# Reciprocal deviation by way of DRAM, and zeros' matmuls at the launch, in an RWKV block

## The chip, the cores and the metric

One core of a Trainium2 chip runs the whole program in one launch. The metric is the device time of that launch in microseconds, the median of several runs.

## The reference

An RWKV block with f32 data on 8 sequences of 256 tokens with 512 channels (32 heads of 16). Cut to what matters:

```
xn = ln(x, ln1_w, ln1_b);  sx = shift(xn) - xn            # shift: the row before, first row from the state
xxx = tanh((xn + sx*maa_x) @ maa_w1)                      # 5 groups of 32
x5  = xn + sx * (maa_stack + xxx @ maa_w2)                # 5 mixed inputs
w   = exp(-exp(time_decay + tanh(x5[1] @ decay_w1) @ decay_w2))
r, k, v = x5[3] @ Wr.T, x5[0] @ Wk.T, x5[2] @ Wv.T;  g = silu(x5[4] @ Wg.T)
for t in tokens:                                          # state s: 16 x 16 per head
    a = k_t v_t^T;  out_t = r_t (u*a + s);  s = a + w_t * s
att = (out - mean) * rsqrt(var + eps) * gn_w + gn_b       # per head of 16 channels
x   = x + (att * g) @ Wo.T
xn2 = ln(x, ln2_w, ln2_b);  sx2 = shift(xn2) - xn2
x   = x + sigmoid((xn2 + sx2*ffn_maa_r) @ Wr2.T) * (relu((xn2 + sx2*ffn_maa_k) @ Wk2.T)**2 @ Wv2.T)
```

## The kernel before

Channels lie on the 128 partitions and tokens along the row; a tile of 128 x 2 x 256 holds half of the 512 channels (`q` is 0 or 1). Each of the 8 batches goes through three functions. `inputs_of_scan` normalizes x, transposes it on TensorE, and makes w, k, v, r and g. `scan` runs the recurrence: v goes to DRAM (`vo`) and is read back in an order that repeats it over partitions (`vs`, line 874), VectorE multiplies it by k (883) and scans (885), GpSimd multiplies by r (888), and TensorE sums over the 16 rows of a state (`gather`, 896). `rest` normalizes per head, multiplies by g, and does the Wo product, the second norm and the feed-forward part.

In `rest` the variance comes out of a TensorE product with a mean matrix (`pv`, 922): the four channel blocks of 128 lie on four groups of 32 partitions, and 32 rows hold the 8 heads of a block, each four times. ScalarE takes the root (927), VectorE the reciprocal (929): `rs`, 128 x 256. Each block's 32 rows must then stand on all four groups of 32 partitions of `att`'s layout. For that ScalarE makes 16 copies of 32 x 256 per batch (lines 948 to 952), into `sqs[1]` (the tile `sq`) for q = 0 and into a tile of the pool `rk` for q = 1. GpSimd multiplies `att` by them (953), ScalarE applies gn_w and gn_b (957), GpSimd multiplies by g (962), and TensorE takes the Wo product. The last batch does the copying with TensorE instead (`psr`, 937).

The launch: x of batch 0 is loaded first, VectorE makes its statistics and the normalized rows (562), TensorE transposes them with the identity `idt` (588), VectorE writes xn from PSUM (595), and ScalarE writes xn * (1 - maa_x) from the same PSUM tile (598), with scale and bias from `ow`, which four small GpSimd operations make in `owners` (517 to 524). VectorE adds the shifted part (622), and TensorE's product with `maa_w1` follows. Between them TensorE centers Wv (`centered_weights`).

The order of all work is written out by hand: `TURNS` gives each piece of each stage a rank, one row for the preparation, then eight rows each for the three functions. `Plan.order` takes pieces by rank as their inputs and buffers come free, gives each a planned start by its own table of costs, and emits the program in the order of these starts. So each engine's queue, and the queue of loads on SyncE (all `dma(...)` calls, line 390), is fixed when the program is built; an instruction at the head of a queue that has to wait holds what is behind it. A few stores are issued from ScalarE's queue (810 and 860).

Of the kernel before, what the change touches and what calls it, by code (L numbers as in the profile page):

```python
# [9 lines left out]
AF = mybir.ActivationFunctionType  # L10
ALU = mybir.AluOpType
# [56 lines left out]
class Plan:  # L68
# [46 lines left out]
    def stage(self):  # L115
# [225 lines left out]
def tile_rwkv_block(  # L341
# [73 lines left out]
    dw1, dw2 = const("dw1", [P, NK, DEC]), const("dw2", [2 * DEC, E])  # L415
    hm = const("hm", [P, NK, 32])
    eh = const("eh", [P, 4])
    ow = const("ow", [P, 2, NK])
    W = {n: [const(f"W{n}{h}", [P, 2, E]) for h in range(2)] for n in "kvrg"}

    pool("s0", 2, [P, NK, S])
# [693 lines left out]
```

## Time and profile before

| | |
|---|---|
| median of 3 runs | 615.86 us (615.41 to 616.64) |
| the profiled execution | 616.02 us, its span 614.2 us |
| TensorE busy | 593.8 us, 97% |
| VectorE, ScalarE, GpSimd busy | 546.0, 515.8, 522.3 us |
| bytes moved by DMA | 124.73 MB, 203 GB/s |
| granted clock of TensorE | 1.00 |

In the profile, L12 is line 12 of the kernel, and the helper `mul` (line 401) issues most matmuls, so that they are told apart by their tiles. Names are written out <- in. In a group of instructions stand the count, the busy time, the mean of one in ns, and the idle time of the engine before them with what ended it. In the timeline stand start, duration, engine, line, operation, tiles, shapes and count. In lists of waits stand the total, the number of times, and the longest. `SPq` and `ACTq` are the queues of SyncE and ScalarE that issue DMAs. A matmul's end is modelled, so TensorE's busy time includes some of its pipeline's tail.

### The profile page before, as it was taken

The page shows a single profiled execution, that of the slowest core. Times are in us where ns is not written, and L with a number is a line of the kernel's source. Part 1 is how long each engine was busy: PE and PEld are TensorE (multiplying, and loading weights), DVE is VectorE, ACT ScalarE, POOL GpSimd, SP SyncE. Part 2 cuts the span into 40 slices and gives each one's busy share as a digit, 9 for nine tenths or more (in the row PEclk, how much of TensorE's full clock was granted, in tenths as well). Part 3 has the DMA queues.
Part 4 walks back from the last instruction along what each step waited for, and adds up shares of the span by engine and source line. Part 5 has one row for each costly group of instructions (what it writes and reads, how often), then busy time and mean ns, then how long its engine had stood idle before and what let it go on. Part 6 is the DMA issues. An engine that isn't in the chain of part 4 may idle for free.

```text
span 614.2 us, 17191 instructions
## 1 busy us (share of the span) xinstructions
PE 593.8 (97%) x7068; PEld 345.9 (56%) x7068; DVE 546.0 (89%) x487; ACT 515.8 (84%) x1171; POOL 522.3 (85%) x421
## 2 busy tenths in 40 slices
PE   4899999899999999999999999999999999999997
PEld 4575656457544764357653885465644474456463
DVE  5789999999999989799898999999999999995432
ACT  4878878999999989999999798999899799966431
POOL 2799999999989999899978999999969998897030
PEclk9999999999999999999999999999999999999999
DMA  8887779568969777867777896796958698681551
GB/s 291 272 199 184 194 186 257 141 176 211 273 174 255 188 187 211 212 201 208 221 188 221 269 230 181 179 273 166 246 142 221 174 257 233 203 238 36 195 186 46
DMA packets 52493, 124.73 MB, mean 203 GB/s; under 512 B 5824, under 2 KB 11200, under 8 KB 52416
## 3 DMA queue, kind: packets, MB, share of 16 engines
q1 hardware_dynamic: 48048, 119.46, 71.2%
q10 hardware_dynamic: 4368, 4.20, 2.2%
q8 instruction: 55, 0.90, 0.7%
q14 instruction: 22, 0.18, 0.1%
HBM read 115.25 MB, written 8.39 MB: 201 GB/s over the span
## 4 chain that ended last, share of the span: by engine, by line
PE 73%; ACT 13%; POOL 5%; DVE 4%; issue 2%; DMA 1%; ACTq 0%; SPq 0%; POOLq 0%; DVEq 0%
PE ps L401 61%; PE ps L896 8%; PE ps L588 2%; ACT att L846 1%; PE ps L760 1%; POOL st L888 1%; ACT wrep L866 1%; POOL mix L720 1%; ACT sq L951 1%; ACT rk L951 1%; DVE st L885 1%; DMA idt<-in_consts 1%; ACT vs L876 1%; ACT att L957 1%; ACT L866 1%
## 5 line engine op out<-in xcount | busy, mean ns | idle before, releaser
L885 DVE TENSOR_TENSOR_SCAN st<-wrep,vs 128x1024 f32<-128x1024 f32 x128 | 289.5, 2280 | 4.1 <-ACT wrep L866 1.0
L888 POOL TENSOR_TENSOR st<-st,r 128x1024 f32<-128x1024 f32 x128 | 254.4, 2001 | 6.2 <-DVE st L885 5.7
L883 DVE TENSOR_TENSOR vs<-vs,ps 128x1024 f32<-128x1024 f32 x122 | 144.2, 1207 | 2.4 <-ACT vs L876 2.1
L401 PE MATMUL ps<-Ws,mix 128*32 128x512 f32 (+1 forms) x864 | 115.0, 589 | 0.8 <-ACT o L986 0.8
L401 PEld LDWEIGHTS ps<-Ws,mix 128*32 128x32 f32 (+1 forms) x864 | 37.4, 116 | 64.8 <-issue 56.9
L720 POOL TENSOR_TENSOR mix<-mix,xn 128x512 f32<-128x512 f32 x62 | 66.7, 1090 | 7.6 <-DVE mix L705 7.6
L896 PE MATMUL ps<-st,con 128*32 128x256 f32 x1024 | 61.6, 380 | 0.9 <-POOL st L888 0.4
L401 PE MATMUL ps<-mix,Wv 128*32 128x256 f32 (+1 forms) x748 | 60.0, 380 | 0.3 <-DVE mix L717 0.3
L401 PE MATMUL ps<-mix,Wr 128*32 128x256 f32 (+1 forms) x616 | 59.2, 380 | 0.6 <-ACT vs L876 0.6
L401 PE MATMUL ps<-mix,Wk 128*32 128x256 f32 (+1 forms) x856 | 58.5, 380 | 0.5 <-DVE x L968 0.3
L401 PE MATMUL ps<-mix,Wg 128*32 128x256 f32 (+1 forms) x712 | 58.6, 379 | 0.0
L401 PE MATMUL ps<-mix,Ws 128*32 128x256 f32 (+1 forms) x688 | 58.0, 380 | 0.0
L401 PE MATMUL ps<-Ws,g 128*32 128x512 f32 (+1 forms) x416 | 56.6, 593 | 0.3 <-POOL g L962 0.2
L610 POOL TENSOR_TENSOR sx<-xn 128x512 f32<-128x512 f32 x31 | 32.3, 1052 | 27.5 <-ACT xn L605 22.5
L635 POOL TENSOR_TENSOR mix<-mix,xn 128x512 f32<-128x512 f32 x44 | 47.6, 1098 | 5.0 <-ACT mix L633 3.8
L846 ACT COPY att<-ps 32x256 f32<-32x256 f32 x128 | 46.7, 365 | 4.4 <-PE ps L838 2.3
L703 ACT ACTIVATE ps<-ps,vec 128x256 f32<-128x256 f32 x112 | 46.8, 443 | 4.1 <-PE ps L401 2.7
L401 PEld LDWEIGHTS ps<-mix,Wv 128*32 128x32 f32 (+1 forms) x748 | 40.2, 120 | 16.9 <-issue 2.3
L401 PEld LDWEIGHTS ps<-mix,Wr 128*32 128x32 f32 (+1 forms) x616 | 40.6, 128 | 16.1 <-POOL mix L720 1.1
L401 PEld LDWEIGHTS ps<-mix,Ws 128*32 128x32 f32 (+1 forms) x688 | 39.9, 123 | 16.1 <-ACT mix L633 0.8
L896 PEld LDWEIGHTS ps<-st,con 128*32 128x32 f32 x1024 | 32.5, 110 | 28.0 <-POOL st L888 4.7
L401 PEld LDWEIGHTS ps<-mix,Wg 128*32 128x32 f32 (+1 forms) x712 | 39.0, 122 | 15.6 <-issue 0.3
(133 smaller groups left out, 968.0 us busy)
## 6 DMA issues: line engine op xcount, KB each, us to landing
vs<-vo SPq DMA_DIRECT2D x128, 512.0 KB, 5.5
Ws<-in_wo SPq DMA_DIRECT2D x16, 512.0 KB, 5.3
Ws<-in_fr SPq DMA_DIRECT2D x16, 512.0 KB, 6.3
Ws<-in_fk SPq DMA_DIRECT2D x16, 512.0 KB, 7.2
Ws<-in_fv SPq DMA_DIRECT2D x16, 512.0 KB, 4.9
x<-in_x SPq DMA_DIRECT2D x9, 512.0 KB, 6.5
vo<-v ACTq DMA_DIRECT2D x15, 256.0 KB, 4.6
out<-o SPq DMA_DIRECT2D x15, 256.0 KB, 4.4
```

Of the source, the lines that this page charges most:

```text
L401: nc.tensor.matmul(out[i : i + n], lhsT=w[:, i : i + n], rhs=x, start=first, stop=final)
L588: nc.tensor.transpose(ps()[:, m, n * P : (n + 1) * P], xh[n]()[:, k * P : (k + 1) * P], idt())
L610: take(512, [sx], [xn], lambda xn=xn, sx=sx, e=nc.vector if quick else nc.gpsimd: e.tensor_tensor(sx(), xn()[:, :, 0:T], xn()[:, :, 1 : T ...
L635: gp(512, t, [t, xn[q]], lambda q=q, t=t: nc.gpsimd.tensor_tensor(t(), t(), xn[q]()[:, :, 1 : T + 1], ALU.add))
L703: act(256, p_, [p_, vec], lambda g=g, q=q, m=m, p_=p_: nc.scalar.activation(p_()[:, m, :], p_()[:, m, :], AF.Identity, bias=col(f"maa_{g}" ...
L720: gp(512, t, [t, xn[q]], lambda q=q, t=t: nc.gpsimd.tensor_tensor(t(), t(), xn[q]()[:, :, 1 : T + 1], ALU.add))
L846: act(350, atts[q], [pc], lambda i=32 * (2 * q + m), m=m, q=q, h=32 * h: nc.scalar.copy(atts[q]()[h : h + 32, m, :], pc()[i : i + 32, 0, :]))
L866: act(4 * T, w, [ew], lambda m=m, w=w, ew=ew: nc.scalar.activation(w()[:, :, 1:T], ew()[:, m : m + 1, 0 : T - 1].to_broadcast([P, 4, T - 1 ...
L883: dve(4 * T, [vs], [vs, kp], lambda m=m, vs=vs, kp=kp: nc.vector.tensor_tensor(vs(), vs(), kp()[:, m : m + 1, :].to_broadcast([P, 4, T]), ...
L885: dve(4 * T, [st], [w, vs], lambda w=w, vs=vs, st=st: nc.vector.tensor_tensor_scan(st().rearrange("p n t -> p (n t)"), w().rearrange("p n ...
L888: gp(4 * T, st, [st, r], lambda m=m, st=st, r=r: nc.gpsimd.tensor_tensor(st(), st(), r()[:, m : m + 1, :].to_broadcast([P, 4, T]), ALU.mul ...
L896: nc.tensor.matmul(pat()[32 * i : 32 * i + 32, 0, :], lhsT=con()[:, s : s + 32], rhs=done[i]()[:, j, :], start=(j == 0), stop=(j == 3),)
```

## The change

Four things. In seven of the eight batches the reciprocal deviation `rs` is stored to a DRAM buffer `rd` from ScalarE's queue, and two loads on SyncE's queue read it back, each repeating 32 rows of 512 values over the four groups of partitions; the 16 copies on ScalarE are gone. At the launch, VectorE writes zeros into one tile and TensorE multiplies them 16 times (128 x 128 by 128 x 256) as its first work, with no reader. In the launch of batch 0, ScalarE makes xn * (1 - maa_x) from VectorE's xn in SBUF instead of from PSUM, with a scale alone, so that `ow` takes one GpSimd operation. All rows of `TURNS` are new.

```diff
-    ow = const("ow", [P, 2, NK])
+    ow = const("ow", [P, NK])
...
+    pool("rd", 2, [32, NK, T], dram)
...
+    warm = plan.pools["xn"][3][1]
+    nc.vector.memset(warm[:, 0, :], 0.0)
     nc.scalar.activation(plan.pools["mn"][1][1], eh()[:, 0:2], AF.Sqrt)
...
+    def warmed():
+        ps = new("ps", "psa")
+
+        def mm():
+            for n in range(16):
+                nc.tensor.matmul(ps()[:, 0, :], lhsT=warm[:, 0, 0:P], rhs=warm[:, 0, 0:T], start=True, stop=True)
+
+        pe(5.8, [ps], [], mm)
+
     def owners():
-        i, j = (VECS.index(v) for v in ("maa_x", "ln1_w"))
-        for n in range(2):
-            gp(4, ow, [vec], lambda n=n: nc.gpsimd.tensor_tensor(
-                ow()[:, n, :], vec()[:, :, j + n], vec()[:, :, i], ALU.mult), 30)
-        for n in range(2):
-            gp(4, ow, [vec, ow], lambda n=n: nc.gpsimd.tensor_tensor(
-                ow()[:, n, :], vec()[:, :, j + n], ow()[:, n, :], ALU.subtract), 30)
+        i = VECS.index("maa_x")
+        gp(4, ow, [vec], lambda: nc.gpsimd.tensor_scalar(ow(), vec()[:, :, i], -1.0, 1.0, ALU.mult, ALU.add), 30)
...
                     t = first[q]
-                    act(256, t, [ps, ow], lambda m=m, k=k, t=t, ps=ps: nc.scalar.activation(
-                        t()[:, m, :], ps()[:, m, :], AF.Identity,
-                        bias=ow()[:, 1, k : k + 1], scale=ow()[:, 0, k : k + 1]), pointers=2)
+                    act(256, t, [xn, ow], lambda m=m, k=k, t=t, xn=xn: nc.scalar.activation(
+                        t()[:, m, :], xn()[:, m, 1 : T + 1], AF.Copy, scale=ow()[:, k : k + 1]), pointers=1)
...
         dve(256, [rs], [rs], lambda: nc.vector.reciprocal(rs()[:, 0:T], rs()[:, 0:T]), 6.25)
+        if not last:
+            rd = new("rd", f"rd{b}")
+            plan.add("ACT", 0.37, [rd], [rs], lambda: nc.scalar.dma_start(
+                out=rd().rearrange("r k t -> k r t"), in_=rs()[:, 0:T]), lag=1.0, kb=131)
...
                 rsb = new("rk", f"rsb{b}_{q}") if q else sqs[1]
-                for n in range(2):
-                    for i in range(4):
-                        rows = slice(32 * i, 32 * i + 32)
-                        act(376, rsb, [rs], lambda blk=2 * q + n, n=n, rows=rows, rsb=rsb: nc.scalar.copy(
-                            by_block(rsb)[rows, n, :], rs()[32 * blk : 32 * blk + 32, 0:T]))
+                dma(rsb, lambda q=q: rd()[:, 2 * q : 2 * q + 2, :].rearrange("r n t -> r (n t)").unsqueeze(0)
+                    .to_broadcast([4, 32, 2 * T]), lambda rsb=rsb: rsb().rearrange("p m t -> p (m t)") if len(rsb().shape) == 3 else rsb(), 262, rd)
...
         load_pairs(W[n], src)
+    warmed()
     owners()
```

More of the change, by code (lines that the diff above doesn't have):

```diff
@@ L538, in normed @@
             mn, nm = new("mn", f"mn{u}"), new("nm", f"nm{u}")
-        if (which == 1 and b > 1) or (which == 2 and b < 5):
+        if (which == 1 and b > (1)) or (which == 2 and b < 5):
             junk = [new("xh", f"xh{u}_{n}") for n in range(NT)]
```

234 rows, old and new, of the table TURNS are left out of this document.

## The prediction

> **What bounds the kernel now.** I read the page first (busy shares, chain), then busy time by stretches, then what TensorE waited for, then the timeline of the launch and of the one place where the removed copies stand next to a wait of TensorE.
>
> ```profile
> span 614.2 us, 17191 instructions
> PE 593.8 (97%) x7068; PEld 345.9 (56%) x7068; DVE 546.0 (89%) x487; ACT 515.8 (84%) x1171; POOL 522.3 (85%) x421
> PE 73%; ACT 13%; POOL 5%; DVE 4%; issue 2%; DMA 1%; ACTq 0%; SPq 0%; POOLq 0%; DVEq 0%
> ...
> 0.00:20.00 20.00, 11.36 (x89) 9.93 (x90) 11.33 (x27) 10.91 (x23) 5.26 (x22) 1.00 0.91 313
> 40.00:60.00 20.00, 19.11 (x317) 11.50 (x319) 19.97 (x18) 15.82 (x37) 20.00 (x16) 1.00 0.85 208
> 100.00:120.00 20.00, 18.01 (x320) 11.16 (x316) 19.53 (x16) 18.97 (x42) 19.68 (x14) 1.00 0.65 172
> 160.00:180.00 20.00, 20.00 (x236) 7.76 (x232) 20.00 (x19) 19.40 (x41) 18.28 (x14) 1.00 0.76 210
> ```
>
> The columns of the last four lines are TensorE, its weight loads, VectorE, ScalarE, GpSimd, then the granted clock. TensorE is the bound once the pipeline is full. In the launch it is nearly half idle; from 40 us on GpSimd and VectorE are as full as it is, so a launch that ends later moves everything behind it. ScalarE is close to full in the middle, but what counts is how often TensorE waited for it:
>
> ```profile
> PE ps L401 <- ACT v L791: 1.3, 1, 1.3
> PE ps L401 <- ACT o L986: 1.2, 2, 0.8
> ...
> PE ps L401 <- ACT vs L876: 0.6, 1, 0.6
> ...
> PE ps L896 <- ACT g L821: 0.4, 1, 0.4
> ...
> PE ps L401 <- ACT tb L768: 0.3, 1, 0.3
> PE ps L838 <- ACT sq L927: 0.3, 1, 0.3
> ...
> PE ps L588 <- ACT xh L572: 0.2, 1, 0.2
> ```
>
> These are all of TensorE's waits for ScalarE after 30 us: 1.3 + 1.2 + 0.6 + 0.4 + 0.3 + 0.3 + 0.2 = 4.3 us. That is the ceiling on what a freer ScalarE gives TensorE directly.
>
> **Launch: zeros' matmuls, and SBUF rows.** The work of the launch:
>
> ```profile
> 0.80 0.06 DVE L463 MEMSET wrep<- 128x4 f32 x1 [0.80 <-PEq L1106]
> ...
> 7.25 1.94 PE L588 MATMUL ps<-idt,xh 128*128 128x128 f32 x8 [7.25 <-DMA idt<-in_consts]
> ...
> 8.44 0.56 ACT L598 ACTIVATE mix<-ps,ow 128x256 f32<-128x256 f32 x1 [0.92 <-PE ps L588]
> ...
> 8.98 4.01 PE L401 MATMUL ps<-Ws,Ws 128*128 128x128 f32 x28
> ...
> 9.04 1.45 DVE L595 TENSOR_SCALAR xn<-ps,vec 128x256 f32<-128x256 f32 x3 [2.57 <-ACT mix L598]
> ...
> 14.94 0.70 PE L401 MATMUL ps<-mix,mw 128*128 128x256 f32 x2 [0.48 <-DVE mix L622]
> ...
> 19.00 1.09 PE L588 MATMUL ps<-idt,xh 128*128 128x128 f32 x8 [0.89 <-ACT xh L572]
> ...
> 19.39 2.96 POOL L711 TENSOR_TENSOR mix<-mix,sx 128x512 f32<-128x512 f32 x2 [2.35 <-ACT mix L709]
> ```
>
> The first eight transposes take 1.94 us, the same eight at 19 us take 1.09: TensorE is slow at first, though the granted clock reads 1.00. A step is about 0.11 us when warm and 0.21 when cold (1.94 and 1.09 less the tail of the last, over seven). The 28 matmuls behind them take 4.01 us, which is about 7 cold steps and 20 warm ones, so the cold stretch is 8 + 7 steps of 0.213 = 3.2 us. The zeros' matmuls are meant to spend that stretch while TensorE waits for the identity's DMA. Their number decides whether they fit:
>
> ```profile
> L838 PE MATMUL ps<-rk,hm 128*32 128x256 f32 x64 | 5.0, 380 | 0.3 <-ACT sq L927 0.3
> L401 PE MATMUL ps<-mix,Wr 128*128 128x256 f32 x136 | 31.4, 382 | 0.0
> L595 DVE TENSOR_SCALAR xn<-ps,vec 128x256 f32<-128x256 f32 x4 | 2.0, 540 | 3.3 <-ACT mix L598 3.3
> L622 DVE SCALAR_TENSOR_TENSOR mix<-xn,vec,mix 128x256 f32<-128x256 f32 x4 | 2.8, 718 | 0.0
> ```
>
> L838 writes four matmuls for each of eight batches, 32, and the trace has 64: a matmul in f32 is two instructions. So the 16 new ones are 32 instructions of the second row's shape, 31.4 / 136 = 0.231 us each when warm, some 0.43 when cold. 3.2 us of cold time hold 7.5 of them, the other 24.5 take 5.7: 8.9 us in all. They start when the zeros are written (VectorE's first work at 0.80, some 0.3 for 256 columns, an estimate from the 4-column row up) at 1.2 and end at 10.1. The identity and the normalized rows are there at 7.25, and TensorE runs its queue in order: the transposes start **2.8 us late**. They then run warm, four of them 0.4 us shorter, so ScalarE and VectorE get their first tile at 8.44 + 2.4 = 10.85.
>
> Against that the chain behind them is shorter. Before, ScalarE's L598 and VectorE's L595 both read the PSUM tile and take turns (VectorE's 2.57 us of idle "<-ACT mix L598"): 8.44 to 14.94, 6.5 us. After, L598 reads the rows that L595 wrote to SBUF, VectorE runs 4 x 0.540 and then 4 x 0.718 = 5.0 us plus handovers, say 5.2, with batch 1's statistics moved behind: 10.85 + 5.2 = 16.05 instead of 14.94, **+1.1 us**. The new turns put ScalarE's two bias copies ahead of batch 1's normalizing (which stands in the 2.35 us that GpSimd waits before 19.39): GpSimd starts earlier by about as much as batch 1's rows come later; I count that as nothing. Three fewer tiny GpSimd operations and the memset are covered by engines that are idle in this stretch (the 0 to 20 us line: GpSimd 5.26, VectorE 11.33). Ends: all 32 warm, 7.4 us, gives −0.4; all 32 cold, 13.8 us, gives +6.0. I stay with the measured 3.2.
>
> [...]
>
> **ScalarE's copies.**
>
> ```profile
> L951 ACT COPY sq<-sq 32x256 f32<-32x256 f32 x56 | 22.5, 402 | 0.7
> L951 ACT COPY rk<-sq 32x256 f32<-32x256 f32 x56 | 22.5, 402 | 1.1 <-DVE sq L929 0.2
> ...
> 108.35 3.66 PE L401 MATMUL ps<-mix,Wr 128*32 128x256 f32 x64 [0.65 <-ACT vs L876]
> ...
> 118.50 0.71 PE L401 MATMUL ps<-tb,mw2b 32*128 32x256 f32 x8 [1.31 <-ACT v L791]
> ```
>
> 112 copies, 45.0 us, leave ScalarE in seven batches (16 x 0.402 = 6.4 each); seven DMA issues come. Of the 4.3 us above, the waits in the stretch right behind a block of copies are 1.3 (v L791, at 118.5) and 0.6 (vs L876, at 108): **−1.9 us**. Ends: 0 (another piece of ScalarE's queue is late next) and −4.3.
>
> **The way over DRAM.** The tightest place is batch 0:
>
> ```profile
> 103.35 1.73 DVE L929 RECIPROCAL sq<-sq 128x256 f32<-128x256 f32 x1
> 105.54 0.40 ACT L951 COPY rk<-sq 32x256 f32<-32x256 f32 x1
> ...
> 112.43 1.64 ACT L951 COPY rk<-sq 32x256 f32<-32x256 f32 x4
> ...
> 115.57 1.11 POOL L953 TENSOR_TENSOR att<-att,rk 128x512 f32<-128x512 f32 x1
> ...
> 121.17 2.35 PE L401 MATMUL ps<-Ws,g 128*32 128x512 f32 x20
> ...
> L888 POOL TENSOR_TENSOR st<-st,r 128x1024 f32<-128x1024 f32 x128 | 254.4, 2001 | 6.2 <-DVE st L885 5.7
> ...
> vo<-v ACTq DMA_DIRECT2D x15, 256.0 KB, 4.6
> out<-o SPq DMA_DIRECT2D x15, 256.0 KB, 4.4
> ...
> SPq L390 <- DMA vo<-v: 51.1, 8, 8.7
> ...
> L876 ACT ACTIVATE vs<-s,cm 128x4 f32<-128x4 f32 x128 | 36.5, 296 | 2.4 <-ACT v L791 0.9 <-DMA vs<-vo 0.9
> ```
>
> Before, the copies run between 105.54 and 114.1, and GpSimd's second multiplication starts at 115.57. After: store issued at 105.5, landed 4.6 later at 110.1, SyncE issues both reads, landed 4.4 to 5 later at 114.5 and 115.5. First data come 2 us later than before, second data about 1.4. Then two multiplications, ScalarE's scale, GpSimd's product by g, and TensorE's Wo. GpSimd is full here (19.68 of 20), so a wait at the head of its queue is lost time, but four of its 2 us products are queued ahead in the new turns and cover most of it. I take **+1.5 us**, between 0 and the 2.6 us that a full landing beyond its cover (5 − 2.4) would cost. In the other six batches the new turns put 15 and more TensorE pieces (eight instructions of 0.231, 1.8 us) between the variance and Wo, 27 us and over, against some 16 us by the steps just walked (103.35 to 119.5): nothing.
>
> [...]
>
> **SyncE's queue.** The reads wait in SyncE's queue until the store has landed, and loads of vs and of weights stand behind them. The trace has eight such holds (vo), 51.1 us, 6.4 each, and they cost ScalarE 0.9 us in all and TensorE nothing (no DMA among its waits after the launch). Seven more at 0.11: **+0.8 us**. Ends: 0, and 7 x 6.4 = 45 with no cover at all. The bytes (4.6 MB on 124.7) are too few to matter.
>
> **The new turns** leave TensorE's order nearly as it was: the same pieces in the same neighbourhood, pairs swapped. I take 0, with 3 us to either side, an estimate: no order can remove more than the waits there are, and 4.3 us of those are the ones above.
>
> **Sum.** +1.1 − 1.9 + 1.5 + 0.8 = +1.5. The profiled execution took 616.02 (614.2 and 1.8 around it), 0.16 over the median: 617.5 in its own terms, **617.4 us** on the median's scale. A measurement of this kernel tells about 0.2% (1.2 us) from no change.
>
> **The rivals.**
> - Faster: ScalarE's 45 us are worth more than its direct waits, since it also feeds VectorE and GpSimd at 18 to 19 of 20. If the 4.3 us go whole and the launch and the round trip come out at their low ends (−0.4 and 0), with the holds at 0.8: −3.9, **612.0 us**. It decides where the relief exceeds launch, trip and holds, 3.4 us. For it: the chain runs 13% through ScalarE. Against it: TensorE at 20.00 of 20 in most stretches.
> - Slower by the queue: SyncE's holds delay weights, which TensorE takes at once. If 0.8 us of each 6.4 us hold comes through, 5.6 instead of 0.8: **622 us**. Against it: TensorE never waited for a weight.
> [...]
> - Nothing shows: the launch's lateness is taken up by waits that stand there anyway (GpSimd's 2.35 us before 19.39), and all else hides: 615.9 us.
>
> **Chances.** Forecast 0.34, cold twice 0.08, queue 0.12; faster 0.36; nothing shows 0.10. So slower by over 0.2%: 0.54, within: 0.10, faster: 0.36. The likeliest's own range is 616.6 to 618.6; to hold 8 in 10 it reaches from 611.5 (the faster case and the turns' spread) to 622.
>
> **What would show it.** The zeros as 32 instructions in TensorE's first row, ending near 10 us; transposes right behind, at the warm step; the last L622 a microsecond later than before; 112 copies gone, ScalarE near 77%; in batch 0 GpSimd idle on the read-back; no wait of TensorE on a weight's DMA. It is wrong if the zeros end before 7.25, or if TensorE's busy pieces after 30 us close up by more than 2 us.

## The result, and the profile after

The changed kernel takes **650.98 us** (median of 4 runs, 648.61 to 652.16); the kernel before took 615.77 beside it. The ratio is 1.057 (95% interval 1.053 to 1.060): 35 us slower, where 1.5 us slower was forecast and 622 was the upper end. The profiled execution took 652.16. Its page: span, busy time by engine, granted clock in 40 slices, the shares of the chain that ended last.

```profile
span 650.4 us, 17360 instructions
PE 612.5 (94%) x7184; PEld 364.8 (56%) x7184; DVE 546.9 (84%) x488; ACT 473.2 (73%) x1061; POOL 522.3 (80%) x418
...
PEclk9999999999999999899997999989999999999999
...
PE 46%; POOL 24%; DMA 14%; ACT 7%; issue 5%; DVE 4%; SPq 0%; ACTq 0%; POOLq 0%; DVEq 0%
```

ScalarE lost its copies (515.8 to 473.2 us), and VectorE and GpSimd do the work they did before (546.9 and 522.3). TensorE, 73% of the chain before, is 46% of it; GpSimd has 24% instead of 5, DMA 14% instead of 1. TensorE is idle 37.9 us of the span instead of 20.4, and busy 18.7 us longer. Of these 18.7, 9.6 are the zeros (below). For the rest, here is busy time in stretches of 100 us, with the granted clock, DMA share and GB/s as the last three columns:

```profile
100.00:200.00 100.00, 94.36 (x1220) 55.01 (x1224) 94.89 (x75) 80.19 (x181) 91.33 (x70) 1.00 0.77 198
200.00:300.00 100.00, 95.94 (x1208) 60.22 (x1204) 88.68 (x75) 82.54 (x194) 88.06 (x73) 0.98 0.78 210
300.00:400.00 100.00, 92.73 (x1124) 53.58 (x1116) 86.51 (x70) 77.52 (x181) 85.92 (x68) 0.97 0.77 209
400.00:500.00 100.00, 92.06 (x1102) 50.60 (x1102) 86.07 (x72) 74.72 (x169) 80.54 (x65) 0.98 0.75 198
500.00:600.00 100.00, 97.32 (x1116) 56.97 (x1112) 89.89 (x74) 68.33 (x144) 88.54 (x66) 0.97 0.73 187
```

The clock was 1.00 throughout before. Here it is 0.98, 0.97, 0.98, 0.97 over four stretches: 2 + 3 + 2 + 3 = 10 us of TensorE's time (an estimate, which counts its idle parts too), about the 9.1 that the zeros leave of the 18.7. What TensorE waits for (line, releaser: total us, times, longest), then who waits for the read-back, and SyncE's queue:

```profile
PE ps L395 <- POOL g L963: 6.1, 1, 6.1
PE ps L395 <- DVE mix L705: 4.2, 2, 4.0
PE ps L838 <- POOL rk L833: 3.5, 1, 3.5
...
PE ps L395 <- DMA Ws<-in_wo: 2.5, 1, 2.5
...
POOL att L954 <- DMA sq<-rd: 18.3, 6, 5.6
ACT vs L876 <- DMA vs<-vo: 14.5, 11, 5.1
POOL att L954 <- DMA rk<-rd: 14.5, 5, 4.5
...
SPq L384 <- DMA rd<-sq: 32.0, 5, 8.5
```

GpSimd's multiplications wait 18.3 + 14.5 = 32.8 us for the two reads. They do so 11 times in 14, not in the first batch alone. GpSimd was nearly full before (18.28 to 20.00 of 20 us from 40 us on, in the lines quoted in the prediction); each of these waits is time it lacks for the products by r and the mixes that TensorE needs. ScalarE's wait for the read-back of v, 0.9 us before, is 14.5. Batch 3 in order of time:

```profile
320.67 1.75 DVE L929 RECIPROCAL sq<-sq 128x256 f32<-128x256 f32 x1 [1.23 <-ACT sq L927]
...
322.45 0.53 ACTq L932 DMA_DIRECT2D rd<-sq  x1
...
331.38 0.54 SPq L384 DMA_DIRECT2D rk<-rd  x1
...
332.02 0.53 SPq L384 DMA_DIRECT2D sq<-rd  x1
...
337.80 1.09 POOL L954 TENSOR_TENSOR att<-att,rk 128x512 f32<-128x512 f32 x1 [2.93 <-DMA rk<-rd]
...
342.51 1.09 POOL L954 TENSOR_TENSOR att<-att,sq 128x512 f32<-128x512 f32 x1 [3.62 <-DMA sq<-rd]
...
347.85 4.66 PE L395 MATMUL ps<-Ws,g 128*32 128x512 f32 x28 [6.06 <-POOL g L963]
```

From the store's issue to the first read's issue pass 8.9 us, from the reads' issue to their data 6.4 and 10.5, and Wo starts 25.4 us after the reciprocal's end, with TensorE idle for 6.06. Its clock is down in the same place (0.50 from 344.00 to 350.83): 340 to 360 us reads 0.83 and TensorE is busy for 13.94 us there. The first line is the same stretch of the kernel before:

```profile
340.00:360.00 20.00, 20.00 (x185) 15.59 (x176) 19.60 (x13) 16.72 (x43) 19.51 (x20) 1.00 0.93 256
...
340.00:360.00 20.00, 13.94 (x156) 4.67 (x152) 12.41 (x14) 12.17 (x32) 17.45 (x14) 0.83 0.79 201
```

Why the reads take so long shows in batch 0, where little else is under way. They are issued at 111.82 and 112.56, Wo's weights at 113.16. Busy time in stretches of one microsecond, the DMA share and GB/s at the end of each line:

```profile
119.00:120.00 1.00, 1.00 (x24) 0.65 (x20) 0.98 (x1) 1.00 (x3) 0.90 (x1) 1.00 0.26 99
120.00:121.00 1.00, 1.00 (x28) 0.58 (x20) 1.00 (x1) 0.98 (x4) 0.00 (x0) 1.00 0.27 103
121.00:122.00 1.00, 1.00 (x24) 0.59 (x20) 1.00 (x3) 0.47 (x1) 0.15 (x1) 1.00 0.26 98
...
121.85 1.09 POOL L954 TENSOR_TENSOR att<-att,rk 128x512 f32<-128x512 f32 x1 [1.95 <-DMA rk<-rd]
```

While GpSimd waits for the second read (119.90 to 121.85), the DMA engines are a quarter busy. I read the share, 0.26 of 16, as four engines at work and twelve with nothing left to do; the trace doesn't name the engine of a packet, but its records of packets fit that. From 113.5 to 115 us the first read has 4.1 to 4.2 packets of 2 KB open at a time. The store of the deviation alone, from 109.5 to 110.5, has 4.1 to 4.3 packets of 1 KB open; the store of v alone, in the kernel before from 108.6 to 109.1, has 16.4 of the same size on average. The read's source has a broadcast of four copies as its outermost dimension, `[4, 32, 512]`, the store's target has `[4, 32, 256]`, and the store of v has 128 rows outermost. That the outermost dimension decides the number of engines is my estimate from these three; no run changed that dimension alone.

Other transfers are late beside the reads. The store of v issued at 112.83 has some 12 packets open beside that read at 114 us, none from 115 on, and its last ones pass between 118 and 121. In batch 3, from 340.5 to 345.5 us, 4.2 packets of 2 KB are open beside 12.3 of 4 KB: read in the same way, twelve engines have gone on to the read-backs of v, while four still work through the reads and, once the second has landed at 342.5, through Wo's weights, which were issued behind them. From 347.5 to 349 us 4.1 packets of 4 KB are left alone.

At the launch, the same view in order of time:

```profile
1.17 9.58 PE L519 MATMUL ps<-xn 128*128 128x256 f32 x32 [1.17 <-DVE xn L457]
...
10.59 1.04 PE L589 MATMUL ps<-idt,xh 128*128 128x128 f32 x8
11.23 1.90 DVE L596 TENSOR_SCALAR xn<-ps,vec 128x256 f32<-128x256 f32 x4 [4.21 <-PE ps L589]
...
15.94 1.13 PE L395 MATMUL ps<-mix,mw 128*128 128x256 f32 x4 [0.32 <-DVE mix L622]
```

The 32 instructions take 9.58 us; the single records step by 0.427 us up to 6.0 and by 0.216 from 6.3 on, so the cold stretch is about 5 us. The transposes behind them run at the warm step, and the second half of the mix starts 1.0 us later than before (15.94 against 14.94).

### The profile page after: what moved, and what is told of

Same layout as the page of the kernel before. It is cut to its first block, busy times and chain, and to the rows that moved or that the text cites. A ratio compares the mean times of both kernels' runs of the same rounds, so it can differ in the third digit from the quotient of the medians.

```text
span 650.4 us, 17360 instructions
## 1 busy us (share of the span) xinstructions
PE 612.5 (94%) x7184; PEld 364.8 (56%) x7184; DVE 546.9 (84%) x488; ACT 473.2 (73%) x1061; POOL 522.3 (80%) x418
## 4 chain that ended last, share of the span: by engine, by line
PE 46%; POOL 24%; DMA 14%; ACT 7%; issue 5%; DVE 4%; SPq 0%; ACTq 0%; POOLq 0%; DVEq 0%
PE ps L395 37%; POOL st L888 11%; DMA sq<-rd 5%; PE ps L896 5%; DMA rd<-sq 4%; POOL mix L720 3%; DMA rk<-rd 3%; POOL att L954 2%; DMA Ws<-in_wo 2%; POOL vs L880 2%; PE ps L519 1%; PE ps L589 1%; POOL mix L635 1%; POOL sx L610 1%; ACT ps L703 1%
## 5 line engine op out<-in xcount | busy, mean ns | idle before, releaser
L395 PE MATMUL ps<-Ws,mix 128*32 128x512 f32 (+2 forms) x864 | 118.3, 598 | 0.2 <-DVE o L1010 0.2
L395 PE MATMUL ps<-Ws,g 128*32 128x512 f32 (+1 forms) x416 | 61.9, 641 | 12.7 <-POOL g L963 6.1
L395 PEld LDWEIGHTS ps<-Ws,mix 128*32 128x32 f32 (+1 forms) x864 | 38.9, 117 | 62.0 <-issue 55.1
L896 PE MATMUL ps<-st,con 128*32 128x256 f32 x1024 | 64.3, 387 | 5.9 <-DVE att L902 2.7
L635 POOL TENSOR_TENSOR mix<-mix,xn 128x512 f32<-128x512 f32 x44 | 47.6, 1097 | 11.4 <-ACT mix L633 10.3
L896 PEld LDWEIGHTS ps<-st,con 128*32 128x32 f32 x1024 | 34.9, 111 | 33.4 <-issue 6.9
L395 PEld LDWEIGHTS ps<-mix,Wv 128*32 128x32 f32 (+1 forms) x808 | 41.6, 117 | 20.2 <-issue 3.5
L395 PEld LDWEIGHTS ps<-Ws,g 128*32 128x32 f32 (+1 forms) x416 | 23.4, 123 | 46.6 <-issue 28.6
L876 ACT ACTIVATE vs<-s,cm 128x4 f32<-128x4 f32 x128 | 36.3, 295 | 17.6 <-DMA vs<-vo 14.5
L705 DVE TENSOR_TENSOR mix<-ps,sx 128x512 f32<-128x512 f32 x56 | 36.8, 683 | 14.2 <-ACT ps L703 13.4
```

What stands on the lines that cost most here:

```text
L395: nc.tensor.matmul(out[i : i + n], lhsT=w[:, i : i + n], rhs=x, start=first, stop=final)
L635: gp(512, t, [t, xn[q]], lambda q=q, t=t: nc.gpsimd.tensor_tensor(t(), t(), xn[q]()[:, :, 1 : T + 1], ALU.add))
L705: dve(512, [t], [p_, sx[q]], lambda q=q, t=t, p_=p_: nc.vector.tensor_tensor(t(), p_(), sx[q](), ALU.mult))
L876: act(4, vs, [s0, cm], lambda i=i, blk=blk, vs=vs: nc.scalar.activation(vs()[:, :, 0:1], s0()[:, blk, 4 * i : 4 * i + 4].rearrange("p (n o ...
L896: nc.tensor.matmul(pat()[32 * i : 32 * i + 32, 0, :], lhsT=con()[:, s : s + 32], rhs=done[i]()[:, j, :], start=(j == 0), stop=(j == 3),)
```

## The experiments

In the expectations, R is the theory that the round trip over DRAM costs the time, T that the new turns do, S that SyncE's holds do; the later names are explained where they stand. Every ratio is to the kernel before on the same chip. The runs stand in three groups: turns and launch, the trip with its waits, the trip's bytes.

**e4: the launch alone**, in the kernel before.

```diff
+            for n in range(16):
+                nc.tensor.matmul(ps()[:, 0, :], lhsT=warm[:, 0, 0:P], rhs=warm[:, 0, 0:T], start=True, stop=True)
...
-                        t()[:, m, :], ps()[:, m, :], AF.Identity,
-                        bias=ow()[:, 1, k : k + 1], scale=ow()[:, 0, k : k + 1]), pointers=2)
+                        t()[:, m, :], xn()[:, m, 1 : T + 1], AF.Copy, scale=ow()[:, k : k + 1]), pointers=1)
```

> The kernel before with the launch of the change alone: 16 zeros' matmuls and ScalarE's rows from SBUF; old turns, copies by ScalarE. By the prediction's launch term +1.1 us: 617 (616 to 619). Theory L: slower by 10 us or more.

617.32 us, ratio 1.0023 (1.0013 to 1.0032): +1.5 us. The launch is a small loss, as the prediction's term had it.

**e5 and e5b: 8 zeros' matmuls instead of 16, and none**, both with the SBUF rows, in the kernel before (`range(16)` to `range(8)`; without `warmed()` and its memset).

> The kernel before with the launch alone, but 8 zeros' matmuls instead of 16: in the trace of after the 16th instruction of the 32 had ended by 7.4 us, about when the normalized rows are ready. By the prediction's launch term without the 2.8 us of lateness: 1 to 2 us faster than before (614 to 615); a launch that others take up: 615.5 to 616.

> The kernel before with only the launch's SBUF rows (ScalarE reads VectorE's result, one GpSimd operation instead of four for the scales), no zeros. With 8 zeros' matmuls beside it the launch was 1.3 us faster than before, with 16 it was 1.5 slower. If the rows carry the gain: about 614.3 to 615. If the warm TensorE carries it: 615.5 to 616.5.

614.45 us with eight (0.9976, 0.9966 to 0.9986) and 615.21 with none (0.9984, 0.9969 to 0.9999). TensorE's launch with eight:

```profile
1.17 6.10 PE L526 MATMUL ps<-xn 128*128 128x256 f32 x16 [1.17 <-DVE xn L464]
7.18 1.06 PE L596 MATMUL ps<-idt,xh 128*128 128x128 f32 x8
```

Eight zeros end about when the identity is there: the transposes start at 7.18 (7.25 before) and run warm, 1.06 us for eight. The launch turns from a loss of 1.5 us into a gain of 1.4, so this version is 0.2% faster than the kernel before. The rows alone gain 0.8; whether the warm array adds to that stays open, since the two intervals overlap.

**e3: the changed kernel without the zeros** (`range(16)` to `range(0)`).

> The kernel after without the zeros' matmuls; all else the same. The zeros ended at 10.6 us and the transposes waited for them: theory L expects 3 us or more back; theories R and T expect 1 to 3 us back (transposes at 7.3 instead of 10.6, but cold), so 648 to 650.

655.75 us (1.0634), 4.8 us slower than with them, where 1 to 3 were expected back. Up to 120 us the stretches behind the launch are as full as in the changed kernel; the time is lost later. GpSimd's waits are much the same (`POOL att L954 <- DMA sq<-rd` 19.6 us, 18.3 in the changed kernel), but TensorE's clock is 0.977 on average over the span instead of 0.984: 15 us of its time instead of 10, a difference of about the 4.8. On its page the lowest slices of the clock are 6, 7 and 8 tenths (from 344, 426 and 491 us), on that of the changed kernel 7, 8 and 8 (from 341, 260 and 423). Why a launch without zeros ends in a lower clock stays open; TensorE's longest wait behind the launch is 7.4 us there and 6.1 in the changed kernel.

**e1: the copies back, in the new turns**; they take ranks 1.5 apart from the store's place on.

```diff
-            plan.add("ACT", 0.37, [rd], [rs], lambda: nc.scalar.dma_start(
-                out=rd().rearrange("r k t -> k r t"), in_=rs()[:, 0:T]), lag=1.0, kb=131)
...
-                dma(rsb, lambda q=q: rd()[:, 2 * q : 2 * q + 2, :] ...
+                for n in range(2):
+                    for i in range(4):
+                        act(376, rsb, [rs], lambda ...: nc.scalar.copy(by_block(rsb)[rows, n, :], ...))
```

> The kernel after, with ScalarE's 16 copies per batch in place of the store and the two reads; zeros, SBUF rows and new turns stay. Theory R (the way over DRAM is the loss: GpSimd's 32.8 us of waits for the read-back at L954, and the cold TensorE behind them): the time falls to 616 to 622 us. Theory T (the new turns are the loss, whatever carries the deviation): it stays above 640. Theory L (the launch): it stays at 650.

664.46 us (1.0787, 1.0766 to 1.0809). This looked like a verdict for T, and was not: TensorE now waits for ScalarE (10.1 us for L986), whose queue I had filled at places of my own choosing. The two runs that follow take the deviation out instead; g3, further down, keeps its waits in the same turns, and settles it.

**f1 and f2: nothing between the reciprocal and the last multiplication**, in the new turns with the new launch (f1) and in those of before (f2): store, reads and copies are left out, and GpSimd multiplies `att` by itself.

```diff
-                    att(), att(), by_block(rsb), ALU.mult))
+                    att(), att(), att(), ALU.mult))
```

> The changed kernel without any work between the reciprocal and the last multiplication: no store, no reads, no copies; GpSimd multiplies the attention by itself, so the deviation isn't applied. Turns, zeros and SBUF rows stay. With the store and the reads in place but nobody waiting on either the kernel took 628.7 us, 13 over the kernel before. Theory Q (those 13 us are the 21 descriptors' slots on SyncE's and ScalarE's queues and their 3.7 MB): about 612 to 618. Theory N (the new turns themselves cost them): about 625 to 630.

> The counterpart in the turns of before: no ScalarE copies, nothing in their place, the attention multiplied by itself. If ScalarE's 112 copies were bearing on the end at all, this is what removing them can bring at most: the prediction took 1.9 us (ends 0 to 4.3), so 611.5 to 616; theory Q and theory N agree here. Below 611 would say that the copies cost more than the prediction allowed.

f1 took 617.79 us (1.0026, 1.0013 to 1.0040), f2 614.84 (0.9982, 0.9971 to 0.9992). So ScalarE's 112 copies were worth 1.2 us, and the new turns cost 617.79 − 616.04 + 1.2 − 1.5 = 1.5 us, if the launch costs in them what it costs in the old ones. Neither makes 35. (The 3.7 MB named in f1's text are the reads' alone; with the store it is 4.6.)

**e2: the trip alone**, in the turns and with the launch of before.

```diff
-                for n in range(2):
-                    for i in range(4):
...
+            plan.add("ACT", 0.37, [rd], [rs], lambda: nc.scalar.dma_start(
+                out=rd().rearrange("r k t -> k r t"), in_=rs()[:, 0:T]), lag=1.0, kb=131)
...
+                dma(rsb, lambda q=q: rd()[:, 2 * q : 2 * q + 2, :] ...
```

> The kernel before with the way over DRAM alone: store and two reads in place of the copies, at the ranks of the copies, old turns and old launch. Theory R: slower than before by 15 us or more (630 to 660), with GpSimd waiting at the first multiplication. Theory T: within 5 us of before (611 to 621), since ScalarE is 45 us freer.

660.31 us (1.072, 1.067 to 1.077). The trip costs 44 us without any new turn. Its waits, by the same view:

```profile
ACT vs L885 <- DMA vs<-vo: 47.5, 12, 13.0
...
POOL att L963 <- DMA rk<-rd: 14.2, 5, 4.6
```

The largest is not GpSimd's for the deviation, but ScalarE's for the read-back of v, a load that the change doesn't touch.

**e6, e7, e8: the changed kernel with one wait or both taken away.** In e6 the reads fetch `x` and not what was stored, so they wait for no store; in e7 GpSimd multiplies `att` by itself, so nobody waits for the reads; e8 does both. All transfers stay. The edit of the reads; that of GpSimd is the one of f1:

```diff
-                dma(rsb, lambda q=q: rd()[:, 2 * q : 2 * q + 2, :].rearrange("r n t -> r (n t)").unsqueeze(0)
+                dma(rsb, lambda q=q: x[b, 32 * q : 32 * q + 32, :].unsqueeze(0)
```

> The kernel after, but the two reads take rows of x in DRAM instead of the stored deviation (same bytes, same 2 KB rows, same place in SyncE's queue; the per-head scale is then wrong): the reads no longer wait for the store. Theory S (the store's landing, 3.3 to 8.9 us after its issue in the trace, holds SyncE's queue and makes the reads late): 616 to 630 us. Theory G (the reads' own landing, 6 to 16 us after their issue, is what GpSimd waits for): above 635. Theory T (the turns as such): 645 or more.

> The kernel after, but GpSimd multiplies att by itself instead of by what was read back (the per-head scale is left out): store and reads stay with all their traffic and their hold of SyncE's queue, nobody waits for the reads. Theory G: 616 to 625 us. Theory S, if it works through the loads held behind the reads: 635 or more. Theory T: 645 or more.

> Both edits at once: reads from x, multiplication by att itself (the per-head scale is left out). The traffic and the new turns are all that is left. If the way over DRAM is the whole loss: 610 to 618 us. If the new turns or the traffic carry part of it, what stands above 616 here is their part.

641.59 us (1.0419), 645.32 (1.0479) and 628.73 (1.021, 1.019 to 1.023). One wait alone gives back 9.4 or 5.7 us, both 22.2. And 628.73 − 617.79 = 10.9 us stay with transfers that nobody waits for. The waits of e8:

```profile
ACT vs L876 <- DMA vs<-vo: 23.0, 12, 6.4
...
PE ps L395 <- DMA Ws<-in_wo: 1.8, 2, 1.5
```

**f3: the same as e8 in the turns and the launch of before.**

> The turns and the launch of before with the trip's store and reads issued but with no wait in them: the reads fetch x, and the attention is multiplied by itself, so the deviation isn't applied. Theory Q (traffic and queue slots cost 13 us): about 625 to 630, as in the new turns. Theory N (they are nearly free, the new turns cost): 612 to 618.

645.45 us (1.0478, 1.0457 to 1.0499), 30.6 over f2. ScalarE's wait for v is 45.6 us there, TensorE's for weights of Wo 7.1. So the mere presence of the transfers costs, and the new turns carry it better than the old.

**g1 and g2: e8 and f3 with a sixteenth of the bytes**: the same 21 transfers at the same places, 8 rows each instead of 128.

```diff
-                out=rd().rearrange("r k t -> k r t"), in_=rs()[:, 0:T]), lag=1.0, kb=131)
+                out=rd()[0:8, 0, :], in_=rs()[0:8, 0:T]), lag=1.0, kb=131)
...
-                    .to_broadcast([4, 32, 2 * T]), ...
+                    .to_broadcast([4, 2, 2 * T]), ...  [0:8]
```

> The changed kernel with the store and the reads issued at their places and with no wait on them, as in the run that took 628.7 us, but each moves 8 rows instead of 128 (a sixteenth of the bytes and packets). The deviation isn't applied. Theory B (the bytes delay the weights and the read-backs of v that other work waits for): back to 617 to 620, as with no transfers at all (617.8). Theory P (the places in the queues cost it, a descriptor's issue and its wait for a buffer): 625 to 630.

> The same cut in the turns and with the launch of before, where the full transfers without a wait took 645.4 us and none at all 614.8. Theory B: 615 to 622. Theory P: 635 to 646.

618.00 us (1.0030, 1.0018 to 1.0041) and 620.86 (1.0075). In the new turns the 21 places in the queues cost 0.2 us and the bytes 10.7; in the old ones 6.0 and 24.6. In g1 the wait for v is back at 2.3 us:

```profile
ACT vs L876 <- DMA vs<-vo: 2.3, 3, 1.1
```

**g3: both waits put back, on the small transfers.**

> The changed kernel with both dependences as they were (the reads wait for the store, GpSimd's multiplications for the reads), but the store and each read move 8 rows instead of 128, so most of the deviation isn't applied. Theory L (the waits themselves cost it, small transfers land little sooner behind the others): 632 to 642, the waits' 22 us nearly whole. Theory B (the waits are long because of the trip's own bytes): 617 to 623, and GpSimd's waits on the reads fall under 10 us in total (32.8 with all rows).

617.17 us (1.0014, 0.9992 to 1.0036): the waits' 22 us are gone too. What is left of them, in the queue of SyncE:

```profile
SPq L384 <- DMA rd<-sq: 23.5, 5, 6.9
```

SyncE is still held 23.5 us by the store, and it costs nothing that shows beside f1 (617.79). None of GpSimd's multiplications waits for a read.

**g4, g6, g7: the store whole; reads of 8 rows, of 64 rows, and of 128 rows with half the columns**, both waits in place.

```diff
-                    .to_broadcast([4, 32, 2 * T]), ...
+                    .to_broadcast([4, 2, 2 * T]), ...  [0:8]
...
+                    .to_broadcast([4, 16, 2 * T]), ... [0:64]
...
+                    .to_broadcast([4, 32, T]), ...     [:, 0:T]
```

> The changed kernel with its store whole and with reads of 8 rows instead of 128, both waits in place; most of the deviation isn't applied. If the reads' bytes carry the loss: 617 to 620. If the store's 1 KB packets carry it: 640 to 651.

> The changed kernel with its store whole and with reads of 64 rows instead of 128, both waits in place; half of the deviation isn't applied. If the loss is in proportion to the reads' bytes: about 630 to 637, half of 33 us over 617. If it begins only where the landing outgrows the 8 to 11 us that the order leaves between a read and its multiplication: nearer to one of the ends, below 625 or above 640.

> The changed kernel with both waits and the store whole; each read brings all 128 rows, but only the first 256 of 512 columns, so as many packets, of 1 KB instead of 2. Half of the deviation isn't applied. If the bytes carry the loss: 620 to 627, as with half the rows (623.4). If the number of packets, or that every DMA engine gets some of each read, carries it: 640 to 651.

618.62 us (1.0042, 1.0022 to 1.0062), 623.40 (1.0124, 1.0044 to 1.0204) and 624.39 (1.0131, 1.0101 to 1.0160). The store's whole bytes cost about 1.4 us (g4 less g3; the intervals overlap). SyncE's hold and the read-back of v in g4:

```profile
SPq L384 <- DMA rd<-sq: 31.5, 5, 9.2
...
ACT vs L876 <- DMA vs<-vo: 1.5, 3, 0.9
```

The hold is as long as in the changed kernel (32.0), and with reads of 8 rows it is nearly free. Half the bytes cost the same by fewer packets or by shorter ones (g6 has two runs, 621.3 and 625.5). And the second half of the bytes costs 28 us where the first cost 5: GpSimd's waits, 32.8 us with whole reads, are

```profile
POOL att L954 <- DMA rk<-rd: 0.9, 2, 0.5
POOL att L954 <- DMA sq<-rd: 0.7, 1, 0.7
```

in g6, and 4.5 us in g7. Half reads land nearly within what the order leaves between a read and its multiplication; whole ones outgrow it. Together:

| kernel | us | step |
|---|---|---|
| before | 616.0 | |
| without the copies (f2) | 614.8 | −1.2 |
| with new launch and turns, nothing in the copies' place (f1) | 617.8 | +3.0 |
| + store and reads of 8 rows, not waited for (g1) | 618.0 | +0.2 |
| + the whole bytes (e8) | 628.7 | +10.7 |
| + the waits (the changed kernel) | 651.0 | +22.3 |
| the waits on reads of 8 rows, the store whole (g4), beside g1 | 618.6 | +0.6 |

Not tried: four transfers of 32 rows, each without the broadcast. By the code, every read that stands in the deviation's place here has the four copies outermost, the small ones too. That four engines carry the reads of the changed kernel is read from its trace (share 0.26, 4.2 packets open); that so few bytes cost so much because of it, that reads without the broadcast would spread over more engines, and that this would bring back the time, is argued. The table also says how much it could be worth: f1, with no trip at all, is 1.8 us slower than the kernel before.

## Why the prediction was wrong

**The step that failed is one sentence under SyncE's queue: "The bytes (4.6 MB on 124.7) are too few to matter."** They are 3.7% of all bytes, and the reads' part of them, 3.7 MB, costs 32 of the 35 us: with reads of a sixteenth, and every other part of the change in place, the kernel takes 618.6 (g4), and 617.2 with the small store too (g3). That the forecast of 617.4 lies beside these is in part luck: it had 2.3 us for the trip and its holds where g4 and g3 stand at +0.8 and −0.6 against f1, and 0.7 too much relief from the copies against 1.5 us of turns that it put at 0. A mean over all bytes was the wrong measure twice. The reads have 4.2 packets open and a share of 0.26, which I take for four of 16 engines; on each of those they are four times the load that the mean has (argued, as said above). And the DMA engines were not idle: the four 20-us lines quoted in the prediction have DMA shares of 0.91, 0.85, 0.65 and 0.76.

Point by point:
- **Launch, +1.1:** right. Alone +1.5 (e4). The zeros end at 10.6 instead of 10.1, since the cold stretch is about 5 us and not the 3.2 of the trace before; the chain behind them is 4.7 us (11.23 to 15.94) and not 5.2, which makes up for it, by luck. The chance "cold twice" (0.08) is that of a cold stretch of 6.4 us, twice the 3.2 of the trace before; no run shows one: it was about 5 us, and the 32 instructions took 9.58 us, and 9.54 in e4, where 10.3 went with it.
- **Copies, −1.9:** −1.2 (f2), in the range 0 to −4.3. It was right to go by waits, 4.3 us, and not by 45 us of busy time.
- **Way over DRAM, +1.5 in batch 0 and nothing in six others:** wrong by far. The landings 4.6 and 4.4 came from transfers of 256 KB; the one of these that stands alone in the trace, the store of v, has 16.4 packets open, and the reads and the store of the deviation have 4.1 to 4.3. Measured: 3.3 to 8.9 us from the store's issue to the read's, then 6.3 to 15.8 to the read's data, so up to 21 us from the reciprocal's end to the data that GpSimd waited for. The "27 us and over" of cover counted TensorE's pieces only; GpSimd has its own queue, and its head stood still 11 times.
- **SyncE's holds, +0.8:** the length of a hold was foreseen well (6.4 us each; five of them, 32.0 in all). Its price depends on the reads: with 31.5 us of hold and small reads g4 takes 618.6, while beside full reads taking the hold away gave back 9.4 us (e6).
- **New turns, 0 ± 3:** +1.5 (f1, less the launch, plus the copies).
- **The rivals:** none of them was it. The slower one put the delay of weights down to SyncE's order; the weights are late in the runs (2.5 us in the changed kernel, 9.2 in e7), but by the bytes: g4 has the same holds and no wait for a weight. A rival "the DMA engines become the bound" was missing; the chain before showed 1% of DMA, which is not the same as room on each engine.
- **What would show it:** the zeros' row, warm transposes, 1 us at the mix and the missing copies are there (ScalarE at 73%, not 77, of a longer span). "No wait of TensorE on a weight's DMA" failed with 2.5 us; "GpSimd idle on the read-back in batch 0" came true (1.95 us), and in the batches behind it too, where it was not foreseen.

## What to carry to other kernels

A transfer is priced by what it does to the transfers around it, not only by its own landing (10.7 us here with nobody waiting for it, e8 less g1): where the DMA engines are as busy as here (shares of 0.73 to 0.78) and loads arrive just in time, ask which engines it uses and what is queued behind it there. Count the packets that each new transfer has open, and look at the outermost dimension of both its ends: with four there it had 4.1 to 4.3 open here, with 128 it had 16.4 (that the dimension is the cause is an estimate). To find whether a trip costs by its waits, its places in queues or its bytes, cut each by itself: small transfers with all waits in place told more here than any wait taken away.

## What was not expected of the hardware

- Behind the reads, whose source has four copies outermost, the DMA share was 0.26 to 0.27 for three microseconds, at 98 to 103 GB/s, while GpSimd waited for two of them. A store with four outermost had 4.1 to 4.3 packets of 1 KB open, one with 128 outermost 16.4.
- TensorE's granted clock fell within a kernel: in the changed one it stands at 0.50 for 3.41 us beside each of four waits (4.0, 2.7, 3.5 and 2.5 us long), beginning between 0.5 us before the wait's end and 1.3 after it, and for 6.83 us around the wait of 6.06 that ends at 347.85. That is 20.5 us at half clock, 10 us of TensorE's time by the estimate above; how much of that is in the 35 can't be told apart from the waits. Waits of 1.5 to 1.7 us in the same trace (ending at 21.50, 113.76 and 192.20) have no such spell, and in f1, where TensorE waits for at most 1.7 us at a time, the mean clock is 1.00.
- Cost is steep in bytes: reads of 1/16, 1/2 and 1 of their size gave 618.6, 623.4 (624.4 by columns) and 651.0 us.
